# A GRU followed by a mixture of experts: shared experts for two blocks at a time, 32x32 turns on VectorE, logits by column groups, first loads in another order

## The chip, the cores and the metric

The kernel runs on one core of a Trainium2 chip. The metric is the device time of one execution in microseconds; smaller is better. The core has five engines that work side by side: TensorE (PE, with its weight loads PEld), VectorE (DVE), ScalarE (ACT), GpSimd (POOL) and SyncE (SP), which issues most DMAs. Each works through its own list of instructions in order, and semaphores make one wait for another.

## The reference, cut to what matters

```python
def cell(h, x):                      # 256 steps, 8 sequences, width 512
    gi = x @ W_ih + b_ih
    gh = h @ W_hh + b_hh
    r = sigmoid(i_r + h_r)
    z = sigmoid(i_z + h_z)
    n = tanh(i_n + r * h_n)
    return (1 - z) * n + z * h
...
x_ = hs.reshape(-1, 512)             # 2048 tokens
probs = softmax(x_ @ w_gate)         # 8 experts, the best 2, their weights made to sum to 1
gu = einsum('th,ehf->etf', x_, w_gate_up)
eo = einsum('eti,eih->eth', silu_and_mul(gu), w_down)
routed = einsum('te,eth->th', combine, eo)
shared = silu_and_mul(x_ @ w_sh_gate_up) @ w_sh_down
return x + (routed + shared)
```

Everything is float32. The GRU is a chain of 256 dependent steps; the experts need only the states.

## The kernel before, in words

Time is cut into 16 blocks of 16 steps (8 sequences x 16 steps = 128 tokens). In each block the 16 steps are issued one after the other, and between a step's last gate and the next step's first gate TensorE is given other work, "pieces" from a queue. A planner at the end of the file gives each piece a cost (`MM = 0.86` for four matmuls of 512 columns or their like) and hands out pieces so that the block's sum is even over its steps. The order on each engine is the order of the program.

A step (`step`, L379 to L418): three gates r, n, z of 16 matmuls each, with the turned state (8 columns) as weights and a 128-column slice of W_hh moving, into four groups of 32 columns of the array. Then VectorE turns each gate's result by 32x32 blocks (L390), ScalarE makes r, nn and z (L398, L406, L409), VectorE makes the new state hT (L402 to L415), GpSimd copies it into `hc` (L418). The input part of the gates ("seeds") is put into the gates' PSUM banks by ScalarE (`open_gate`, L366).

The other work:
- `project` (L283, tile gip): x @ W_ih of a later block, 12 pieces a block. The result gi gets its bias on VectorE (L321), goes to DRAM, and comes back in another layout, four steps at a time, as the seeds (`load_seeds` L350, `turn_seeds` L354).
- `transpose_x` (L270, tile xTp): x of a later block turned by four full 128x128 transposes on TensorE, copied by ScalarE (L272).
- `shared_unit` (L670, tile gu_s): the shared experts of the block before. Four units a block, each four "up" pieces (16 matmuls of 32 weight columns and 128 moving tokens), a gate on ScalarE and VectorE (L598 to L600), two "down" pieces (L283, tile po).
- routing of the block before: `choose` (L430, tile lgp: logits, 128 weight columns, 8 moving columns), `order_experts`, `weigh`, `give_places` (L483, L485), `enter` (indirect DMAs into lists), `send_rows` (L523, tile hrp: the states turned back on TensorE, copied by ScalarE, sent to DRAM).

After the last step the last block's shared experts run while the lists of tokens are finished (the shared tail), and then 39 tiles of 128 tokens go through the chosen experts (L606, L742), each gathered and added back by indirect DMAs.

At the start x of block 0 comes by ScalarE's queue, W_ih in three 1 MB DMAs and W_hh in four by SP's, and the two biases spread over 128 partitions by GpSimd's queue; then block 0 is projected, its seeds go to DRAM and back, and the first step starts.

Of the kernel before, what the change touches and what calls it, by code (L numbers as in the profile page):

```python
# [17 lines left out]
P = 128  # L18
TS = 16
SC = 4  # L20
NS = 2
# [4 lines left out]
def kernel(  # L26
# [45 lines left out]

    nc = tc.nc
# [21 lines left out]
    three = ctx.enter_context(tc.tile_pool(name="three", bufs=2))  # L95
# [3 lines left out]
    ps_t = ctx.enter_context(tc.tile_pool(name="ps_t", bufs=1, space=PSUM))  # L99
    ps_o = ctx.enter_context(tc.tile_pool(name="ps_o", bufs=1, space=PSUM))  # L100
# [3 lines left out]
    x_tiles = {}  # L104

    def load_x(k, queue=nc.sync):
        xt = xpool.tile([P, D], F32, tag="x", name=f"x_{k}")
        queue.dma_start(xt, x[:, k * TS : (k + 1) * TS, :])
        x_tiles[k] = xt

    load_x(0, nc.scalar)
# [4 lines left out]
    whh = we[:, E - 4 : E - 2].rearrange("p e w n -> p (e w n)").rearrange("p (q n) -> p q n", q=NQ)  # L116
    for g in range(3):
        nc.sync.dma_start(
            wih[:, :, g * D : (g + 1) * D],
            w_ih[:, g * D : (g + 1) * D].rearrange("(q p) n -> p q n", p=P),  # L120
        )
    bias = const.tile([P, G3], F32, name="bias")
    nc.gpsimd.dma_start(bias, b_ih.partition_broadcast(P))
    bias_h = we[:, 0, 0:2].rearrange("p w n -> p (w n)")
    nc.gpsimd.dma_start(bias_h, b_hh[0 : 2 * D].partition_broadcast(P))
    h = state.tile([P, NQ, 32], F32, name="h")
    nc.vector.memset(h, 0.0)
    h0v = h0.rearrange("b (q j i) -> b j q i", q=NQ, j=4)
    for j in range(4):
        nc.gpsimd.dma_start(h[32 * j : 32 * j + B], h0v[:, j])  # L130
    for q in range(NQ):
        nc.sync.dma_start(whh[:, q, :], w_hh[q * P : (q + 1) * P, :])
    load_x(1)
    wg = wts.tile([P, NQ, E], F32, name="wg")
# [7 lines left out]
    def load(tile_, src):  # L142
        loads.append(lambda: nc.gpsimd.dma_start(tile_, src))

    def load_shared():
        load(wg, w_gate.rearrange("(q p) e -> p q e", p=P))
        up = w_sh_gate_up.rearrange("(q p) (two c f) -> p q two c f", p=P, two=2, f=IM)
        down = w_sh_down.rearrange("(c f p) n -> c p f n", p=P, f=NF)
        for c in range(NSH):
            for two_i in range(2):  # L150
                for q in range(0, NQ, 2):
                    load(wsu[c][:, q : q + 2, two_i, :], up[:, q : q + 2, two_i, c, :])
            for f in range(NF):
                load(wsd[c][:, f, :], down[c][:, f, :])

    def load_expert(e):
        for q in range(NQ):
            load(we[:, e, q, :], w_gate_up[e, q * P : (q + 1) * P, :])
        for f in range(NF):
            load(we[:, e, NQ + f, :], w_down[e, f * P : (f + 1) * P, :])  # L160
# [26 lines left out]
    def counting(name, n, base, step, channel):  # L187
# [24 lines left out]


# [8 lines left out]
    nc.vector.tensor_tensor(  # L222
        bias[:, 0 : 2 * D], bias[:, 0 : 2 * D], bias_h, ALU.add
    )
    b_hn = b_hh[2 * D : G3].rearrange("(q j i) -> j q i", q=NQ, j=4)
    for j in range(4):
        nc.gpsimd.dma_start(
            seed_hn[32 * j : 32 * j + B].rearrange("p (q i) -> p q i", i=32),
            b_hn[j].partition_broadcast(B),
        )  # L230
# [9 lines left out]
    nc.gpsimd.dma_start(listed[0 : E * NM], vacant)  # L240
    nc.gpsimd.dma_start(listed[E * NM : E * NM + 1], vacant[0:1])
# [13 lines left out]
    by_groups = [True]  # L255
    spare = deque()

    def for_transposes(shape, name):

        if by_groups[0]:  # L260
            return ps_t.tile([P, *shape], F32, tag="tp", name=name)
# [5 lines left out]
    def transpose_x(k):  # L267
        ps = for_transposes([NQ, P], f"xTp_{k}")
        for q in range(NQ):
            nc.tensor.transpose(ps[:, q, :], x_tiles[k][:, q * P : (q + 1) * P], ident)  # L270
        xT = two.tile([P, NQ, P], F32, tag="xrT", name=f"xT_{k}")
        nc.scalar.copy(xT, ps)  # L272
        xT_of[k] = xT
        x_tiles.pop(k)
# [3 lines left out]
    def multiply(ps, lhs, rhs, start, stop):  # L278


        for c in range(4) if by_groups[0] else (slice(0, P),):
            rows_ = slice(32 * c, 32 * c + 32) if by_groups[0] else c
            nc.tensor.matmul(  # L283
                ps[rows_], lhs[:, rows_], rhs, start=start, stop=stop, skip_group_check=True
            )

# [18 lines left out]
    def project(k, g):  # L305
# [3 lines left out]
        def issue(q, cols):  # L309
            if q == 0 and cols.start == 0:  # L310
# [3 lines left out]
                xT_of[k][:, q, :],  # L314
# [5 lines left out]
        def end():  # L320
            nc.vector.tensor_tensor(  # L321
                gi[:, :, g, :].rearrange("p j (q i) -> p j q i", i=32),
                box["ps"].rearrange("p (q j i) -> p j q i", j=4, i=32),
                bias[:, g * D : (g + 1) * D].rearrange("p (q j i) -> p j q i", j=4, i=32),
                ALU.add,
            )
            if g > 0:
                to = gi_dram[k][g % 2].rearrange("j b t n -> (b t) j n")
                if g == 1:
                    nc.sync.dma_start(to.rearrange("p j (a n) -> p j a n", a=2), gi[:, :, 0:2, :])  # L330
                else:
                    nc.sync.dma_start(to, gi[:, :, 2, :])
                    projected.add(k)
# [9 lines left out]
    def load_seeds(c):  # L343

        k, o = divmod(c * SC, TS)
        assert k in projected
        steps = slice(o, o + SC)
        for tile_, src in zip((seeds_n, seeds[c % NS]), gi_dram[k]):
            for j in range(4):
                nc.sync.dma_start(tile_[32 * j : 32 * j + B], src[j, :, steps, :])  # L350
    def turn_seeds(c):
# [16 lines left out]
    whh_v = whh.rearrange("p q (a j i) -> p q a j i", j=4, i=32)  # L368
    hc_of = {}

# [566 lines left out]
```

## Time and profile before

| what | us |
|---|---|
| median of 3 runs (lowest, highest) | 1541.06 (1536.35, 1541.35) |
| profiled execution, its own time | 1539.5 |
| its span, from first to last instruction | 1537.7 |
| first step's first gate starts at | 35.46 |
| last step's first gate starts at | 1262.83 |
| first matmul for the last block's logits | 1267.21 |
| first transposition of a token tile | 1295.81 |

The span is what the trace covers; the profiled execution's time lies 1.8 us above it. A row of the stage view gives a stretch, its length, each engine's busy time with the count of instructions, the granted TensorE clock (1.00 is full), the share of DMA time and GB/s. A line of the timeline gives start, duration, engine, line, operation and tiles, shapes and count, and in brackets the idle time before and what ended it. A matmul's record is 0.27 us or longer, since matmuls overlap: what one costs is the distance between starts, not its duration. A float32 matmul appears as two instructions. In places the records are displaced by a few instructions, so that the last ones of one group bear the next group's name.

### The profile page before, as it was taken

To read this page: it belongs to the slowest core of one execution; us is meant where nothing else is said; L and a number is where in the kernel's file an instruction comes from. 1 tells how busy PE (TensorE), PEld (TensorE's weight loads), DVE (VectorE), ACT (ScalarE), POOL (GpSimd) and SP (SyncE) were. 2 spreads that over 40 slices of the span, in tenths; PEclk is the share of its full clock that TensorE was granted. 3 is DMA by queue.
4 is the path that set the end of the run, shared out by engine and by line. 5 is a ranking of instruction groups with operands and counts; after the bars stand their busy time and mean duration, and the time that the engine had idled before them with its cause. 6 is when DMAs were issued, how large, how long until landed. Compare 5 with 4: busy or idle time off the path is not lost.

```text
span 1537.7 us, 82219 instructions
## 1 busy us (share of the span) xinstructions
PE 1472.1 (96%) x36779; PEld 1156.5 (75%) x36779; DVE 732.9 (48%) x2747; ACT 435.5 (28%) x1799; POOL 253.7 (16%) x492
## 2 busy tenths in 40 slices
PE   4999799999999999999999999999999999999996
PEld 1777678887889897879897979797889886444442
DVE  2555354545455555555555555555455553222221
ACT  1332232333233323333323333333233331222221
POOL 2112111111110000000001010101010213444442
PEclk9999999999999999999999999999999999999998
DMA  7334122322221111111111110101010224455453
GB/s 255 91 104 105 29 55 50 81 49 82 48 61 29 45 32 45 32 39 31 40 37 30 40 41 22 48 21 48 21 48 22 70 64 142 85 94 90 89 96 48
DMA packets 52720, 94.51 MB, mean 61 GB/s; under 512 B 9152, under 2 KB 25616, under 8 KB 52368
## 3 DMA queue, kind: packets, MB, share of 16 engines
q0 software_dynamic: 16416, 41.00, 12.7%
q1 hardware_dynamic: 35816, 47.99, 11.2%
q8 instruction: 290, 4.75, 1.3%
q14 instruction: 62, 0.51, 0.1%
q10 hardware_dynamic: 136, 0.26, 0.1%
HBM read 57.85 MB, written 31.37 MB: 58 GB/s over the span
## 4 chain that ended last, share of the span: by engine, by line
PE 94%; issue 2%; DMA 1%; DVE 1%; ACT 0%; SPq 0%; POOLq 0%; POOL 0%; DVEq 0%; ACTq 0%
PE ps_r L379 15%; PE ps_n L379 15%; PE gu_s L670 15%; PE ps_z L379 15%; PE gip L283 11%; PE gu_t L606 9%; PE po L283 7%; PE yp L742 4%; PE lgp L430 1%; DMA x<-in_x_dram 1%; PE xTp L270 1%; PE hrp L523 1%; PE ps_r L723 0%; PE ps_z L723 0%; PE ps_n L723 0%
## 5 line engine op out<-in xcount | busy, mean ns | idle before, releaser
L379 PE MATMUL ps_r<-we,hT 128*8 128x128 f32 x8192 | 292.7, 274 | 15.4 <-ACT ps_r L366 9.1
L379 PE MATMUL ps_z<-we,hT 128*8 128x128 f32 x8192 | 295.0, 273 | 6.8 <-issue 6.2
L379 PE MATMUL ps_n<-we,hT 128*8 128x128 f32 x8192 | 295.8, 273 | 4.7 <-issue 4.2
L379 PEld LDWEIGHTS ps_r<-we,hT 128*8 128x8 f32 x8192 | 240.5, 90 | 73.9 <-issue 30.1
L670 PE MATMUL gu_s<-hc,wsu 128*32 128x128 f32 x8192 | 280.7, 275 | 10.3 <-issue 10.0
L670 PEld LDWEIGHTS gu_s<-hc,wsu 128*32 128x32 f32 x8192 | 252.5, 111 | 30.9 <-issue 22.1
L379 PEld LDWEIGHTS ps_z<-we,hT 128*8 128x8 f32 x8192 | 241.2, 90 | 11.8 <-issue 10.8
L379 PEld LDWEIGHTS ps_n<-we,hT 128*8 128x8 f32 x8192 | 240.7, 90 | 11.0 <-issue 9.3
L418 POOL COPY hc<-hT 128x32 f32<-128x32 f32 x256 | 62.2, 243 | 1076.1 <-DVE hT L415 1076.1
L398 ACT ACTIVATE r<-rT 128x32 f32<-128x32 f32 x256 | 58.6, 229 | 566.7 <-DVE rT L390 564.5
L390 DVE STREAM_TRANSPOSE rT<-ps_r 128x128 f32<-128x128 f32 x256 | 81.0, 316 | 264.5 <-PE ps_r L379 263.5
L283 PE MATMUL gip<-we,xT 128*32 128x512 f32 (+1 forms) x1904 | 190.6, 517 | 1.5 <-ACT xT L272 1.5
L390 DVE STREAM_TRANSPOSE nT<-ps_n 128x128 f32<-128x128 f32 x256 | 81.2, 317 | 144.3 <-PE ps_n L379 144.2
L606 PE MATMUL gu_t<-we,xrT 128*128 x312 | 146.7, 593 | 0.2 <-ACT xrT L725 0.2
L283 PE MATMUL po<-wsd,act_s 128*32 128x512 f32 (+2 forms) x1108 | 138.4, 539 | 1.7 <-DVE act_s L600 1.7
L283 PEld LDWEIGHTS gip<-we,xT 128*32 128x32 f32 x1904 | 58.9, 110 | 67.6 <-issue 56.5
L366 ACT COPY ps_n<-seed_hn 128x128 f32<-128x128 f32 x256 | 68.9, 269 | 104.5 <-DVE nT L390 103.4
L390 DVE STREAM_TRANSPOSE zT<-ps_z 128x128 f32<-128x128 f32 x256 | 81.1, 317 | 18.2 <-PE ps_z L379 10.4
L599 DVE TENSOR_TENSOR act_t<-gu_t,act_t 128x256 f32<-128x256 f32 x39 | 16.6, 425 | 146.3 <-ACT act_t L598 146.3
L606 PEld LDWEIGHTS gu_t<-we,xrT 128*128 128x128 f32 x312 | 53.3, 190 | 38.7 <-issue 38.0
L406 ACT ACTIVATE nn<-nt 128x32 f32<-128x32 f32 x256 | 58.8, 229 | 82.8 <-DVE nt L404 80.5
L748 POOL DMA_INDIRECT out_dram<-y,row x39 | 61.5, 1578 | 124.7 <-DVE y L745 111.1
(162 smaller groups left out, 1231.8 us busy)
## 6 DMA issues: line engine op xcount, KB each, us to landing
gid_rz<-gi SPq DMA_DIRECT2D x16, 512.0 KB
seeds<-gid_rz SPq DMA_DIRECT2D x256, 32.0 KB
we<-in_L_ffn_w_gate_up_dram POOLq DMA_DIRECT2D x32, 256.0 KB, 3.7
gid_n<-gi SPq DMA_DIRECT2D x16, 256.0 KB
seeds_n<-gid_n SPq DMA_DIRECT2D x256, 16.0 KB
wsu<-_L_ffn_w_sh_gate_up_dram POOLq DMA_DIRECT2D x16, 256.0 KB, 3.2
rows<-hr SPq DMA_DIRECT2D x16, 256.0 KB
again<-in_x_dram SPq DMA_DIRECT2D x16, 256.0 KB
```

The source lines that it names most:

```text
L283: nc.tensor.matmul(ps[rows_], lhs[:, rows_], rhs, start=start, stop=stop, skip_group_check=True)
L366: nc.scalar.copy(banks[g][:, 0:P], src[g])
L379: nc.tensor.matmul(bank[32 * j : 32 * j + B, 0:P].rearrange("p (a i) -> p a i", i=32), hT[:, q, 0:B], whh_v[:, q, lo : lo + NQ, j, :], sta ...
L390: nc.vector.transpose(gT.rearrange("p a b -> p (a b)"), banks[g][:, 0:P])
L398: nc.scalar.activation(r, gr, AF.Sigmoid)
L406: nc.scalar.activation(nn, nt, AF.Tanh)
L418: nc.gpsimd.tensor_copy(hc_of[k].rearrange("p q (b t) -> p q b t", t=TS)[:, :, :, t], new)
L599: nc.vector.tensor_tensor(act, ps[:, 0:IM], act, ALU.mult)
L606: nc.tensor.matmul(box["ps"], lhs(q), w_up(q), start=(q == 0), stop=(q == NQ - 1))
L670: nc.tensor.matmul(box["ps"][32 * g : 32 * g + 32, m, :], wsu[c][:, q, two_i, fs], hc_of[k][:, q, :], start=(m == 0 and q == 0), stop=(q = ...
L742: nc.tensor.matmul(box["y"], lhs, rhs, start=(f == 0), stop=(f == NF - 1))
L748: nc.gpsimd.indirect_dma_start(out=out.rearrange("b t d -> (b t) d"), out_offset=bass.IndirectOffsetOnAxis(ap=laid["row"][:, i : i + 1], a ...
```

## The change

- Shared experts run for a pair of blocks: `hc` holds two blocks, an up piece has 256 moving tokens, there are eight units a pair, each half of the former in weights, issued four in each of the two following blocks. The down pieces of a unit are issued after the up pieces of the second unit after it (`down_later`), with three buffers for act and two PSUM banks for po. The last pair runs after the last step.
- x and the states are turned by VectorE in 32x32 blocks. For that, the width is split as (j, q, i) instead of (q, j, i), by strided DMAs of x, W_ih, W_hh, w_gate, w_sh_gate_up and rows in parts of 16 or 32 partitions (`by_turns`, `by_state`), x and rows in runs of 512 bytes.
- The logits are made by four matmuls side by side, one for each q, each with 32 weight columns (w_gate, filled with zeros), and summed by a second, small matmul one step later (`sum_logits`). `give_places` goes by column groups too.
- The first loads: x first, in eight parts on two queues, W_ih by gates, x of block 1 before W_hh, W_hh by gates. The lists' first values are written from the queue of loads. Biases are loaded as one row and spread by a matmul with a row of ones. The first four projection pieces of block 1 go ahead of the first step.

```diff
-    load_x(0, nc.scalar)
+    load_x(0, (nc.sync, nc.scalar))
...
+    nc.scalar.dma_start(bias_row, b_ih.unsqueeze(0))
+    nc.scalar.dma_start(bias_h, b_hh[0 : 2 * D].unsqueeze(0))
     for g in range(3):
...
+        for ps, src in by_state(w_ih[:, cols]):
+            nc.sync.dma_start(wih[ps, :, cols], src)
...
+    def spread_bias(g):
+        ps = ps_mm.tile([P, D], F32, tag="mm", name=f"biasp_{g}")
+        cols = slice(g * D, (g + 1) * D)
+        nc.tensor.matmul(ps, one, bias_row[:, cols], start=True, stop=True)
+        nc.scalar.copy(bias[:, cols], ps)
...
     def transpose_x(k):
-        ps = for_transposes([NQ, P], f"xTp_{k}")
-        for q in range(NQ):
-            nc.tensor.transpose(ps[:, q, :], x_tiles[k][:, q * P : (q + 1) * P], ident)
-        xT = two.tile([P, NQ, P], F32, tag="xrT", name=f"xT_{k}")
-        nc.scalar.copy(xT, ps)
+        xT = two.tile([P, NG, NQ, 32], F32, tag="xrT", name=f"xT_{k}")
+        nc.vector.transpose(
+            xT.rearrange("p g q s -> p (g q s)"), x_tiles.pop(k).rearrange("p g m -> p (g m)")
+        )
...
         for q in range(NQ):
-            nc.tensor.matmul(ps, hc[:, q, :], wg[:, q, :], start=(q == 0), stop=(q == NQ - 1))
-        lg = two.tile([P, E], F32, tag="lg", name=f"lg_{k}")
-        nc.scalar.copy(lg, ps)
+            nc.tensor.matmul(
+                ps[32 * q : 32 * q + 32, 0:P], wg[:, q, :], hc[:, :, q, :], start=True, stop=True
+            )
+        parts = two.tile([P, P], F32, tag="parts", name=f"parts_{k}", bufs=1)
+        nc.scalar.copy(parts, ps[:, 0:P])
+        lg_of[k] = ps, parts
+
+    def sum_logits(k):
+        ps, parts = lg_of[k]
+        multiply(ps[:, P : P + E], columns(parts), sel, start=True, stop=True)
...
-        for q in range(NQ):
-            nc.tensor.transpose(ps[:, q * P : (q + 1) * P], hc[:, q, :], ident)
-        hr = two.tile([P, D], F32, tag="y", name=f"hr_{k}")
-        nc.scalar.copy(hr, ps)
-        nc.sync.dma_start(rows[:, k * TS : (k + 1) * TS, :], hr)
+        hr = two.tile([P, NG, P], F32, tag="y", name=f"hr_{k}")
+        nc.vector.transpose(
+            hr.rearrange("p g m -> p (g m)"), hc_of_block(k).rearrange("p g q s -> p (g q s)")
+        )
+        for ps, dst in by_turns(rows, k):
+            nc.sync.dma_start(dst, hr[ps])
...
-                        box["ps"][32 * g : 32 * g + 32, m, :],
+                        box["ps"][32 * g : 32 * g + 32, two_i, :],
                         wsu[c][:, q, two_i, fs],
-                        hc_of[k][:, q, :],
+                        hc_of[m][:, :, q, :],
...
-        quota = 2.8 * PROJECT if k == 0 else sum(p[0] for p in projections) / max(1, NB - 1 - k)
+        quota = 33 * MM if k < 2 else sum(p[0] for p in projections) / max(1, NB - 1 - k)
...
-        if k > 0:
-            for c in range(NSH):
-                feed_at_once(shared_unit(k - 1, c, NSH))
+        if k > 1:
+            half = NSH * NF // 2
+            for u in range(half):
+                feed_shared(k // 2 - 1, half * (k % 2) + u)
...
-    for c in range(NSH):
-        feed_at_once(shared_unit(k, c, NSH))
+    for u in range(NSH * NF):
+        feed_shared(k // 2, u)
+    while down_later:
+        queue.extend(down_later.popleft())
```

## The prediction

> **What bounds the kernel now.** I read the page first: TensorE is busy almost all of the span and the chain of waits is TensorE for 94%.
>
> ```profile
> span 1537.7 us, 82219 instructions
> ...
> PE 1472.1 (96%) x36779; PEld 1156.5 (75%) x36779; DVE 732.9 (48%) x2747; ACT 435.5 (28%) x1799; POOL 253.7 (16%) x492
> ...
> q8 instruction: 290, 4.75, 1.3%
> ...
> PE 94%; issue 2%; DMA 1%; DVE 1%; ACT 0%; SPq 0%; POOLq 0%; POOL 0%; DVEq 0%; ACTq 0%
> ```
>
> The reader is to see that fewer TensorE microseconds should be a shorter span, unless something else waits behind TensorE. To look for that I cut the span into stages: start-up to 35.46, sixteen blocks of 16 GRU steps to 1262.83 plus a last step, the shared tail to 1295.8, the expert tiles.
>
> ```profile
> 35.46:111.00 75.54, 74.74 (x1880) 54.37 (x1884) 37.71 (x139) 24.72 (x103) 14.27 (x32) 0.98 0.31 93
> 111.00:199.36 88.36, 77.17 (x2233) 65.02 (x2226) 40.69 (x163) 23.17 (x104) 18.19 (x34) 0.98 0.29 66
> 199.36:1195.80 996.44, 982.88 (x29167) 842.27 (x29167) 533.90 (x2101) 307.92 (x1363) 89.35 (x259) 1.00 0.17 42
> 1195.80:1262.80 67.00, 63.81 (x2042) 56.45 (x2035) 36.54 (x151) 21.93 (x98) 11.85 (x29) 1.00 0.29 76
> 1267.20:1295.80 28.60, 26.76 (x550) 19.27 (x551) 9.67 (x43) 2.59 (x8) 12.54 (x18) 1.00 0.57 164
> 1295.80:1537.70 241.90, 227.28 (x703) 110.77 (x701) 63.12 (x118) 52.28 (x117) 97.29 (x75) 0.98 0.47 83
> ```
>
> Columns: stretch and length, busy PE, PEld, DVE, ACT, POOL, then clock, DMA share, GB/s. The 996.44 row holds the 208 steps of blocks 2 to 14, 4.79 each; block 15 (67.00, fifteen steps) has less other work and takes 4.47 a step. Block 1 (88.36) has TensorE idle for 11.2 us. The timeline of one step in the middle gives the law:
>
> ```profile
> 900.43 1.06 PE L379 MATMUL ps_r<-we,hT 128*8 128x128 f32 x32
> 901.31 1.06 PE L379 MATMUL ps_n<-we,hT 128*8 128x128 f32 x32
> 902.18 1.06 PE L379 MATMUL ps_z<-we,hT 128*8 128x128 f32 x32
> 903.05 1.90 PE L283 MATMUL gip<-we,xT 128*32 128x512 f32 x16
> ...
> 904.27 0.19 DVE L415 TENSOR_TENSOR hT<-nn,hn 128x32 f32<-128x32 f32 x1
> ...
> 904.77 1.06 PE L379 MATMUL ps_r<-we,hT 128*8 128x128 f32 x32
> ```
>
> Three gates start 0.87 apart, 2.62 in all; two projection pieces fill 1.72 (0.86 each); the new state was there at 904.46, before the fill ended. A step is 2.62 + F, F being the fill. In block 15 F is only 1.3:
>
> ```profile
> 1243.41 1.06 PE L379 MATMUL ps_z<-we,hT 128*8 128x128 f32 x32
> ...
> 1244.28 1.50 PE L670 MATMUL gu_s<-hc,wsu 128*32 128x128 f32 x48
> 1244.53 0.32 DVE L390 STREAM_TRANSPOSE zT<-ps_z 128x128 f32<-128x128 f32 x1
> ...
> 1245.50 0.19 DVE L415 TENSOR_TENSOR hT<-nn,hn 128x32 f32<-128x32 f32 x1
> ...
> 1245.83 1.06 PE L379 MATMUL ps_r<-we,hT 128*8 128x128 f32 x32
> ```
>
> From 1241.66 to 1245.83 the step is 4.17: TensorE waits for hT. So a step is max(2.62 + F, 4.17), and fill below 1.55 buys nothing. This floor decides the case.
>
> [...] 0.873 / 8 = 109 ns per set of four column groups at N = 128, 0.86 / 2 = 430 at N = 512. [...] steps whose fill has a full-array piece (xTp, hrp) run 0.3 us over the law. [...] TensorE stops for 2 to 4 us inside a run with no wait shown ("issue"). [...] here 0.711 for 128x512 (seeds_n row).
>
> **The change, part by part.** I count against the profiled execution (span 1537.7, time 1539.5, so 1.8 around it; 1.6 under the median 1541.06).
>
> *Shared experts, two blocks at once.* 16 matmuls of 256 columns take the place of two sets of 128. [...] the trace, 109 at 128 and 430 at 512, gives 215 to 218. That is 2% of 8192 x 27.3 ns = 224 us, below 5 us; I take 0 and keep -5. An up piece now lasts 1.72 and is still booked at 0.86, so fill gets uneven.
>
> *Full-array work leaves TensorE.* Per block: xTp 4 x 0.107 + 0.3 = 0.73, gone; hrp 0.73, gone; lgp 1.25 [...] becomes four 128-column matmuls side by side, 0.22, and eight of 8 columns, 0.2 at most; posp 0.28 becomes 0.2. Fifteen times (0.73 + 0.73 + 0.83 + 0.08) = 35.5 us of fill less. In their place VectorE gets two 0.711 turns a block, and ACT two 0.58 copies fewer. The turns stand behind hT on VectorE; what is queued behind them is rT of the next step, due 1.06 after its r gate starts, with 0.56 to spare before nt. One turn fits in that; with gi (0.69) or gated work (0.84) ahead, or the seeds' turn beside weigh (0.91), it can pass it. Bounds: 0 to 1 us a block; I take 0.35, 5 us in all.
>
> *Moved work.* Block k's shared experts wait for the pair: one block (24 x 0.86 = 20.6) and 3.0 of late down pieces go from under the GRU into the tail. Four projection pieces (3.4) go ahead of the first step. Fill falls by 35.5 + 20.6 + 3.0 + 3.4 = 62.5, from 514 to 452.
>
> *What the floor gives back.* The changed kernel's instruction order on TensorE, built, gives the fill after each step. In blocks 6 to 14 it is 1.53, 1.07, 1.31, 1.31, 1.51, 1.75, 2.62, 1.31, 2.19, 2.19, 2.19, 2.62, 1.31, 2.19, 2.19, 1.31: eight of sixteen under 1.55. Filling them up to the floor costs 1.9 a block, 3.5 in block 2, 4 in block 15: 31 us over the kernel, against 3 before (block 15 alone). So the GRU gains 62.5 - 28 = 34.5.
>
> *Stalls.* The law gives 1178 for the 1227.4 from first to last step start; 49 are stalls, 15 of them in block 1, where wsu's loads meet the eight list entries. The loads stay; block 1 now has only 512-column pieces, 16 matmul instructions in 1.72 instead of 64, so fewer to fetch, and x and rows go in 512-byte pieces, eight DMAs instead of one. With VectorE's 5 I take 42, range 27 to 60.
>
> *SP's queue.* Per block 32 seed loads of 0.33 stay, x and rows grow from 2 issues to 16: 5 us more in a 72 us block. Seeds are fetched a chunk of four steps (17 us) ahead; hidden.
>
> *Start-up.* Now x lands at 11.84 behind 3 MB of W_ih and 1.3 MB of spread biases, the projection runs 13.7 to 26.4, and the round trip of the seeds lasts to 35.46:
>
> ```profile
> 11.98 1.08 PE L270 MATMUL xTp<-ident,x 128*128 128x128 f32 x4 [8.20 <-DMA x<-in_x_dram]
> ...
> 27.19 0.37 SPq L332 DMA_DIRECT2D gid_n<-gi  x1
> ```
>
> Changed: x first, biases as two rows, W_ih by gates. 1.3 MB less and one gate (1 MB) instead of three before the first matmul: I put the start at 7 to 8. Twelve pieces 10.3, three bias matmuls 2.6[...]: end about 22.5; the four moved pieces to 26. The seeds of r and z: gi at 19, then 0.4 + 2.96 + 1.3 + 2.2 as today: 26. First step 26.5, 9 earlier (bounds 23 and 31). n's seeds come about 2 late for step 0, as the first step's 2.7 stall now.
>
> *Tail.* Pieces before the first tile: 16 up of 1.72 and 20 down of 0.86 = 44.7, choose, places, lists 2.1; waits 2 (3.3 now; the longer cover should hide some): 48.8 against 28.6, +20.2. Tiles unchanged, 241.9.
>
> Sum: -34.5 - 7 (stalls) - 9 + 20.2 = -30; span 1507, time **1508**.
>
> **Rivals.** *More gain:* the stalls fall to 27, start 3 us earlier, the 5 us of the longer matmuls come: 1485. For it: instruction fetch has less to do, and no mode switch is left. Against: half the steps stand on the floor and would keep what is gained under them. *Slower, by one mechanism:* VectorE's queue between hT and the next rT lengthens the chain, so that the floor is 4.5 instead of 4.17. The same sum with 4.5 gives 44 us more, 1552; it decides from 4.43 on (33 us more). For it: the added turns, and eight steps a block with no slack. Against: order_experts and weigh (1 us of VectorE) already stand there and cost nothing in filled steps; block 15 lost only 0.3 in such steps. *No change:* floor near 4.4, 1537, because what leaves TensorE was cover. *The change doesn't do what it says:* the longer moving operand alone brings next to nothing, as above; my forecast already says that the gain is from the removed full-array work and the start.
>
> **How the numbers follow.** Forecast 1508 (1493 to 1523): 0.62. More gain: 0.22. Floor near 4.4: 0.06. Floor 4.5 and over: 0.10. The range 1484 to 1536 holds the first two and the better part of the third. A measurement can't tell less than 0.3% (4.6 us) from none: faster 0.86, same 0.04, slower 0.10.
>
> **What would show it.** Right: first r gate near 26; no xTp and hrp; unfilled steps of 4.2 and filled ones at the law; blocks of 72 to 75; gu_s near 218 ns per set of 256 columns; tail near 49. Wrong: unfilled steps at 4.4 or more with rT late, blocks 0 and 1 above 85, or a first step after 31.

## The result, and the profile after

The changed kernel took 1515.51 us in the median of 4 runs (1514.79 to 1517.33), the kernel before 1539.19 (4 runs, three of them those of the table above, 1536.35 to 1541.35): a ratio of 0.985, 95% interval 0.983 to 0.987. It is about 24 us faster, where the forecast had 33 under the earlier median, 31.5 under the profiled execution. The kernel before is less steady from one measurement to another than within one: beside the experiments its median was 1521 to 1535. The profiled execution took 1514.91, its span is 1513.1.

These lines of the page after answer to those shown of before: span, engines, instruction fetch (packets, MB, share), the chain by engine.

```profile
span 1513.1 us, 75290 instructions
...
PE 1443.1 (95%) x33154; PEld 1058.3 (70%) x33154; DVE 751.6 (50%) x2782; ACT 423.4 (28%) x1786; POOL 258.6 (17%) x505
...
q8 instruction: 261, 4.28, 1.2%
...
PE 90%; DMA 3%; DVE 3%; issue 2%; ACT 1%; SPq 0%; ACTq 0%; POOLq 0%; DVEq 0%; POOL 0%
```

TensorE has 3625 instructions and 29 us less. Its share of the chain fell from 94% to 90%, and DMA and VectorE have 3% each instead of 1%: something ahead of TensorE has become longer. The stage view says where (stretch and length; busy PE, PEld, DVE, ACT, POOL; clock, DMA share, GB/s). The stretches are block 0, block 1, blocks 2 to 14, block 15 up to its last step, the tail from the last block's logits on, and the tiles:

```profile
55.06:126.31 71.25, 71.25 (x1895) 57.19 (x1891) 40.37 (x144) 20.82 (x96) 19.15 (x45) 1.00 0.39 107
126.31:204.06 77.75, 74.66 (x1883) 58.44 (x1878) 42.88 (x163) 21.40 (x100) 21.89 (x42) 1.00 0.42 89
204.06:1154.76 950.70, 932.69 (x25941) 747.26 (x25938) 541.20 (x2116) 297.82 (x1352) 89.76 (x259) 1.00 0.15 41
1154.76:1219.99 65.23, 62.39 (x1808) 51.08 (x1809) 37.40 (x151) 21.52 (x98) 12.19 (x30) 1.00 0.28 73
1224.38:1271.60 47.22, 47.13 (x701) 23.56 (x701) 14.69 (x54) 3.80 (x12) 12.61 (x18) 1.00 0.41 116
1271.60:1513.10 241.50, 227.33 (x703) 110.92 (x702) 63.11 (x118) 52.33 (x117) 97.35 (x75) 0.98 0.48 84
```

The first number matters most: the first gate starts at 55.06, where it was 35.46 before and 26.5 in the forecast. Everything behind it went as forecast or better:

| stretch (us) | before | forecast | after | after less forecast |
|---|---|---|---|---|
| start to first r gate | 35.46 | 26.5 | 55.06 | +28.6 |
| first to last step's start | 1227.4 | 1185.9 | 1164.9 | -21.0 |
| last step's start to last logits | 4.4 | 4.4 | 4.4 | 0 |
| logits to first tile | 28.6 | 48.8 | 47.2 | -1.6 |
| tiles | 241.9 | 241.9 | 241.5 | -0.4 |
| span | 1537.7 | 1507.5 | 1513.1 | +5.6 |

So a time 7.5 us from the forecast hides two errors of 20 to 30 us with opposite signs. (The forecast's own parts add up to a span of 1507.5, a time of 1509.3 with the 1.8 around it; the 1508 written there is 1.3 short of its sum.) The start is read from the timeline of the changed kernel (start, duration, engine, line, operation, tiles, in brackets the idle time before and its releaser):

```profile
10.74 5.35 PE L310 MATMUL gip<-we,xT 128*32 128x512 f32 x24 [6.82 <-DMA we<-in_L_cond_W_ih_dram]
...
20.11 8.94 SPq L152 DMA_DIRECT2D we<-in_L_cond_W_hh_dram  x12
...
23.00 0.69 DVE L356 TENSOR_TENSOR gi<-gip,bias 128x512 f32<-128x512 f32 x1 [3.93 <-PE gip L310]
...
29.93 8.69 SPq L119 DMA_DIRECT2D x<-in_x_dram  x8
38.73 0.40 SPq L366 DMA_DIRECT2D gid_rz<-gi  x1
...
48.03 0.71 DVE L391 STREAM_TRANSPOSE nT<-seeds_n 128x512 f32<-128x512 f32 x1 [19.72 <-DMA seeds_n<-gid_n]
48.67 0.67 DVE L299 STREAM_TRANSPOSE xT<-x 128x512 f32<-128x512 f32 x1
...
49.48 5.76 PE L310 MATMUL gip<-we,xT 128*32 128x512 f32 x32 [22.00 <-DVE xT L299]
...
55.06 1.06 PE L419 MATMUL ps_r<-we,hT 128*8 128x128 f32 x32
```

gi of r and z is complete at 23.7, but its DMA to DRAM is issued only at 38.73: on SP's queue the twelve parts of W_hh (20.11 to 29.05) and the eight parts of x of block 2 (29.93 to 38.62) stand ahead of it. Of the 8.69 us of x 6.9 are waiting for an earlier DMA to land, as the waits of SP's queue show (us in total, times, longest); of the 8.94 of W_hh it is 3.2:

```profile
SPq L119 <- DMA we<-in_L_cond_W_hh_dram: 6.9, 8, 1.0
```

Then comes the round trip; and VectorE turns n's seeds before x of block 1, so that the four moved projection pieces run alone, from 49.48 on, and the first gate waits for them. They take 5.76 us. TensorE stood still for 22.00 before them, and its granted clock, 1.00 in each us up to 29, is 0.50 from 30 to 53 and 1.00 again from 54 on; the pieces' weight loads start 0.86 apart up to 53.73 and 0.43 apart at their end.

The weights themselves came late too. The same stage view for 10 to 20 us, of before:

```profile
10.00:20.00 10.00, 7.35 (x44) 2.37 (x48) 1.85 (x4) 0.59 (x1) 2.51 (x5) 1.00 1.04 390
```

and after:

```profile
10.00:20.00 10.00, 9.26 (x54) 2.46 (x58) 0.82 (x2) 0.59 (x1) 0.00 (x0) 1.00 1.03 206
```

The DMA engines are as busy (1.04 and 1.03), but move 206 GB/s instead of 390. Packets of 2048 bytes took 84 ns in the median of this stretch before and 165 ns after. The changed kernel loads the two matrices in parts of 32 partitions, the kernel before over all 128, a difference that the prediction did not price. Whether it is the cause had to be tried.

In the steps the floor stayed where it was. A step of block 8 after, with 1.3 us of fill, in the timeline:

```profile
649.29 1.06 PE L419 MATMUL ps_r<-we,hT 128*8 128x128 f32 x32
650.16 1.06 PE L419 MATMUL ps_n<-we,hT 128*8 128x128 f32 x32
651.03 1.06 PE L419 MATMUL ps_z<-we,hT 128*8 128x128 f32 x32
651.90 0.23 PE L310 MATMUL lgp<-sel,parts 128*32 128x8 f32 x8
651.97 1.06 PE L310 MATMUL gip<-we,xT 128*32 128x256 f32 x16
653.46 1.06 PE L419 MATMUL ps_r<-we,hT 128*8 128x128 f32 x32 [0.44 <-DVE hT L455]
```

From 649.29 to 653.46 it is 4.17, the floor of before, and TensorE's last wait is for hT: VectorE's added turns did not lengthen the chain. By the law of the prediction, max(2.62 + F, 4.17), the steps after add up to 1144.2; they took 1164.9, so that the stalls are 20.7, where they were 49 and 42 had been forecast.

### The profile page after: what moved, and what is told of

Same layout as the page of the kernel before. It is cut to its first block, busy times and chain, and to the rows that moved or that the text cites. A ratio compares the mean times of both kernels' runs of the same rounds, so it can differ in the third digit from the quotient of the medians.

```text
span 1513.1 us, 75290 instructions
## 1 busy us (share of the span) xinstructions
PE 1443.1 (95%) x33154; PEld 1058.3 (70%) x33154; DVE 751.6 (50%) x2782; ACT 423.4 (28%) x1786; POOL 258.6 (17%) x505
## 4 chain that ended last, share of the span: by engine, by line
PE 90%; DMA 3%; DVE 3%; issue 2%; ACT 1%; SPq 0%; ACTq 0%; POOLq 0%; DVEq 0%; POOL 0%
PE ps_r L419 16%; PE ps_n L419 15%; PE gu_s L705 15%; PE ps_z L419 14%; PE gu_t L659 9%; PE gip L310 9%; PE po L310 7%; PE yp L785 4%; DMA we<-in_L_cond_W_hh_dram 1%; DVE zT L430 1%; DMA we<-in_L_cond_W_ih_dram 1%; DVE hn L454 0%; ACT z L449 0%; DVE hT L455 0%; PE ps_z L766 0%
## 5 line engine op out<-in xcount | busy, mean ns | idle before, releaser
L419 PEld LDWEIGHTS ps_r<-we,hT 128*8 128x8 f32 x8192 | 226.1, 89 | 119.3 <-ACT ps_z L403 72.7
L419 PE MATMUL ps_r<-we,hT 128*8 128x128 f32 x8192 | 280.8, 273 | 18.4 <-DVE hT L455 11.3
L419 PE MATMUL ps_n<-we,hT 128*8 128x128 f32 x8192 | 288.6, 273 | 1.0 <-issue 0.4
L419 PE MATMUL ps_z<-we,hT 128*8 128x128 f32 x8192 | 283.7, 273 | 2.4 <-issue 2.4
L705 PE MATMUL gu_s<-hc,wsu 128*32 128x256 f32 x4096 | 250.6, 379 | 1.2 <-issue 1.1
L419 PEld LDWEIGHTS ps_n<-we,hT 128*8 128x8 f32 x8192 | 233.6, 90 | 8.3 <-issue 7.5
L310 PE MATMUL gip<-we,xT 128*32 128x512 f32 (+1 forms) x1976 | 197.2, 508 | 29.5 <-DVE xT L299 22.0
L705 PEld LDWEIGHTS gu_s<-hc,wsu 128*32 128x32 f32 x4096 | 150.9, 110 | 76.0 <-issue 14.6
L310 PE MATMUL po<-wsd,act_s 128*32 128x256 f32 (+1 forms) x1408 | 137.9, 476 | 0.0
L310 PEld LDWEIGHTS gip<-we,xT 128*32 128x32 f32 x1976 | 73.7, 111 | 82.0 <-issue 63.9
```

What stands on the lines that cost most here:

```text
L310: nc.tensor.matmul(ps[32 * c : 32 * c + 32], lhs(c), rhs, start=start, stop=stop, skip_group_check=True,)
L419: nc.tensor.matmul(bank[32 * j : 32 * j + B, 0:P], hT[:, q, 0:B], whh_v[:, q, a, j, :], start=False, stop=(q == NQ - 1), skip_group_check= ...
L705: nc.tensor.matmul(box["ps"][32 * g : 32 * g + 32, two_i, :], wsu[c][:, q, two_i, fs], hc_of[m][:, :, q, :], start=(two_i == 0 and q == 0) ...
```

## The experiments

Three questions: what makes the first gate late, why the steps lost more stalls than forecast, and whether the floor is what it seemed. "First gate" is the start of the first r gate. Single executions are read by their stages; times measured apart are compared by their ratio to the kernel before, which ran beside each. The first two experiments, the up pieces of 128 tokens and the dummy work were measured beside one another (before 1533.36), so were the two queues, the later turn, the full booking and the two together (before 1521.39), and so were the run over all partitions and the last one (before 1535.46).

### Start: block 0's gi and seeds on GpSimd's queue

```diff
-                    nc.sync.dma_start(to.rearrange(...), gi[:, :, 0:2, :])
+                    (nc.gpsimd if k == 0 else nc.sync).dma_start(to.rearrange(...), gi[:, :, 0:2, :])
...
-                nc.sync.dma_start(tile_[32 * j : 32 * j + B], src[j, :, steps, :])
+                (nc.gpsimd if c < NS else nc.sync).dma_start(tile_[32 * j : 32 * j + B], src[j, :, steps, :])
```

> The changed kernel, but block 0's gi and its first two chunks of seeds go by GpSimd's queue instead of SP's. Theory A (place in SP's queue: gi of z was ready at 23.7 us and its DMA was issued at 38.7, behind the issues of W_hh and of two x blocks): the seeds of r and z are there near 31, the first r gate starts near 31 to 36 instead of 55. Theory B (the loads themselves are slow: 32 partitions at a time, 160 to 206 GB/s in the start-up windows against 290 to 390 before): W_hh still lands near 38, so the gates of the first step are held apart by W_hh, n and z not before 33 and 38; the first step ends near 40. If A alone holds, the second step starts by 37; if B holds too, near 41. Either way 14 to 20 us less in all, about 1496 to 1501.

Measured: 1505.75 (before 1533.36), first gate 52.76. gi now leaves SP's queue out, as the timeline shows:

```profile
24.46 0.83 POOL L366 DMA_DIRECT2D gid_rz<-gi  x1 [17.56 <-DVE gi L356]
...
35.02 2.05 POOL L386 DMA_DIRECT2D seeds<-gid_rz  x4 [9.73 <-DMA gid_rz<-gi]
...
42.31 0.27 ACT L403 COPY ps_r<-seeds 128x128 f32<-128x128 f32 x1 [14.72 <-DMA seeds<-gid_rz]
```

It is issued 14.3 us earlier, but lands only at 35, after 10.5 us, while the DMA engines are full with W_hh and x (share 1.07 from 30 to 40 us); in the changed kernel it lands by 41.6, 3 us after its issue. The seeds of r and z then take 7.3 us by this queue until ScalarE copies them (42.31), against 3.6 by SP's (41.64 to 45.21). The first gate gains 2.3 us, not 19 or more: a miss. Getting out of SP's queue does not by itself free the step. How much the place in the queue costs with an equally fast queue this run doesn't tell.

### Start: W_ih and W_hh over 128 partitions in one DMA each

```diff
-        for ps, src in by_state(w_ih[:, cols]):
-            nc.sync.dma_start(wih[ps, :, cols], src)
+        src = w_ih[:, cols].rearrange("(j q i) n -> q j i n", j=4, i=32)
+        for q in range(NQ):
+            nc.sync.dma_start(wih[:, q, cols], src[q])
```

and the same for W_hh.

> The changed kernel, but W_ih and W_hh are loaded by 128 partitions at a time (one DMA for each gate and q, same bytes, same number of DMAs, same 2 KB runs), nothing else moved. Theory B [...]: 10 to 30 us shows 350 GB/s and more instead of 200, W_hh is there by about 24 instead of 38, SP's issues are held up less, and the first step starts near 38 to 42 instead of 55. Theory A alone (only the order of issues on SP matters, the number of issues is the same): GB/s as before and first step within 3 us of 55.

Measured: 1550.13, first gate 92.87. A miss, and not a test of what was meant. The stage view for 10 to 20 us:

```profile
10.00:20.00 10.00, 7.52 (x34) 1.51 (x34) 1.99 (x7) 1.87 (x2) 0.00 (x0) 1.00 0.26 98
```

A DMA share of 0.26 is the time of 0.26 x 16 = 4.2 engines, and j, the first dimension of each source here, has 4 values. The run of the next section has as many DMAs, as large and over as many partitions, with 128 successive rows as the source, and a share of 0.70 and 225 GB/s in the same stretch. So the rate goes with the form of the source; what in it does so was not shown, that it is j is an estimate from the 4.2. A packet of 2048 bytes took 87 ns, first evidence for the partitions, though with a quarter of the engines' time in use.

### Start: as many DMAs of the same size, over all partitions

```diff
-        for ps, src in by_state(w_ih[:, cols]):
-            nc.sync.dma_start(wih[ps, :, cols], src)
+        for q in range(NQ):
+            nc.sync.dma_start(wih[:, q, cols], w_ih[q * P : (q + 1) * P, cols])
```

and the same for W_hh.

> The changed kernel with W_ih and W_hh loaded by 128 contiguous rows at a time (one DMA for each gate and group of 128 rows: twelve DMAs of 256 KB for each matrix, as many and as large as in the changed kernel, with the same 2 KB runs, each DMA over all 128 partitions instead of 32). Rows of the two matrices stand in another order than the states expect, so the recurrence computes with permuted weights; sizes, counts and order of all work are unchanged. Theory A (a DMA into 32 partitions moves at half the rate): 2 KB packets take about 86 ns instead of 164, 350 to 400 GB/s in 10 to 20 us, gi of the r gate on its way by 30, first r gate at 38 to 46 instead of 55, whole time 1499 to 1508. Rival B (the number of DMAs and SP's waits for the DMA eight earlier set the pace, whatever their partitions): about 200 GB/s in 10 to 20 us, first r gate at 53 or later, time 1514 to 1517.

Measured: first gate 46.27, 8.8 us earlier; time 1509.27 (before 1535.46). 2 KB packets took 84 ns, and 337 GB/s were moved from 18 to 24 us (212 from 21 to 30 after); from 20 to 30 it is 270 at a DMA share of 0.79, where the changed kernel has 193 at 0.92. The timeline of this run:

```profile
8.84 5.35 PE L310 MATMUL gip<-we,xT 128*32 128x512 f32 x24 [4.91 <-DVE xT L299]
...
23.31 6.46 SPq L119 DMA_DIRECT2D x<-in_x_dram  x8
...
29.89 0.40 SPq L366 DMA_DIRECT2D gid_rz<-gi  x1
...
39.39 0.71 DVE L391 STREAM_TRANSPOSE nT<-seeds_n 128x512 f32<-128x512 f32 x1 [13.08 <-DMA seeds_n<-gid_n]
40.02 0.67 DVE L299 STREAM_TRANSPOSE xT<-x 128x512 f32<-128x512 f32 x1
...
40.84 5.62 PE L310 MATMUL gip<-we,xT 128*32 128x512 f32 x32 [15.37 <-DVE xT L299]
...
46.27 1.06 PE L419 MATMUL ps_r<-we,hT 128*8 128x128 f32 x32
```

gi's DMA is issued 8.84 earlier, and all behind it moves along: 2.0 of this is gi itself (z added by 21.7 instead of 23.7), 6.8 the shorter wait on SP's queue. With number, size, queue and order of the DMAs the same, and 2 KB packets in both, the partitions of each differ, and with them the rows that it reads: the half rate is shown, and costs 8.8 us at the start. Theory A held, the sizes were a little too hopeful (46.27 against at most 46; the time is 1.3 over its range, and block 1 took 81.5 in this execution instead of 77.8). The expected 350 to 400 GB/s in 10 to 20 us did not come (225): W_ih had landed by 15.5, and W_hh was issued only from 16.54 on.

### Start: the two halves of the partitions on two queues

```diff
-        for ps, src in by_state(w_ih[:, cols]):
-            nc.sync.dma_start(wih[ps, :, cols], src)
+        for j, (ps, src) in enumerate(by_state(w_ih[:, cols])):
+            (nc.sync if j < 2 else nc.scalar).dma_start(wih[ps, :, cols], src)
```

and the same for W_hh.

> The changed kernel, but of W_ih's and W_hh's parts the upper two groups of 32 partitions (64 to 127) go by ScalarE's queue and the lower two by SP's, side by side; the parts themselves are unchanged. Theory B [...]: the window 10 to 20 us shows 330 GB/s and more instead of 206, W_hh is there by about 24 instead of 38, gi's DMA for r and z is issued near 26 instead of 38.7, first r gate 36 to 42 instead of 55, in all 13 to 18 us less (near 1500). Rival (runs of 2 KB in parts of 256 KB are slow by their size, whatever partitions): GB/s within 20% of 206, first gate within 4 us of 55.

Measured: 1500.68 (before 1521.39), first gate 50.78 instead of 36 to 42. The rate hardly rose. The stage view of the changed kernel for 20 to 30 us:

```profile
20.00:30.00 10.00, 7.48 (x52) 1.68 (x44) 1.38 (x2) 1.17 (x2) 0.00 (x0) 1.00 0.92 193
```

and of this run for 10 to 20 and 20 to 30:

```profile
10.00:20.00 10.00, 7.73 (x50) 2.14 (x54) 0.33 (x1) 0.00 (x0) 0.00 (x0) 1.00 0.86 184
20.00:30.00 10.00, 3.50 (x18) 0.83 (x14) 1.00 (x2) 2.07 (x3) 0.00 (x0) 0.78 0.98 244
```

In the stretch that the forecast named, 10 to 20, it is 184 instead of the expected 330 (206 in the changed kernel). From 22 to 28, where W_hh lands and the engines are full in both, it is 244 against 222 (323 in the run over all partitions). So two DMAs of 32 partitions side by side, one in each half, did not do here what one over all 128 does. And ScalarE's copies of the bias now stand behind its issues of W_hh:

```profile
25.76 1.28 ACT L260 ACT_TABLE_LOAD   x1 [25.76 <-DMA we<-in_L_cond_W_hh_dram]
27.05 0.59 ACT L260 COPY bias<-biasp 128x512 f32<-128x512 f32 x1
```

and gi of z, which needs the bias, is added at 32.5 instead of 23.7; its DMA leaves at 34.34. A miss in rate and first gate; the time fell near its forecast, but the kernel before was shorter here as well, and the ratio of this one execution, 0.986, shows no gain over 0.985. The issues were put ahead of work on ScalarE that I had not counted.

### Start: in addition, n's seeds turned behind x and the four pieces

```diff
-    turn_seeds(0)
-    load_seeds(1)
     load_shared()
...
     for g in banks:
         open_gate(0, g)
+    turn_seeds(0)
+    load_seeds(1)
```

> e5_two_queues, and VectorE's turn of n's first seeds goes behind the turn of x of block 1 and the four moved projection pieces, which it stood ahead of. Theory C (in the changed kernel the four pieces waited for that turn, 49.5 to 55, so that they were on the way to the first step instead of beside it): the pieces run right behind block 0's projection, first r gate near 29 to 33, the second step's r gate near 34 to 37, 4 to 6 us less than e5_two_queues. Rival (x of block 1 comes late anyway): within 2 us of e5_two_queues.

Measured: 1494.52, first gate 42.09, 8.7 earlier than with the two queues alone. The timeline:

```profile
37.81 0.70 DVE L299 STREAM_TRANSPOSE xT<-x 128x512 f32<-128x512 f32 x1
...
38.66 3.64 PE L310 MATMUL gip<-we,xT 128*32 128x512 f32 x32 [1.59 <-DVE xT L299]
...
42.09 1.08 PE L419 MATMUL ps_r<-we,hT 128*8 128x128 f32 x32
```

The pieces start while the seeds of n are still on their way, and take 3.64 instead of 5.76; their weight loads start 0.43 apart, and the granted clock is 1.00 from 40 to 50 us, where it was 0.50 in the changed kernel. The order on VectorE (with the next seeds' loads, which move along with the turn) is worth 8.7 us of the first gate here, and 6.2 us of the time. The gate came 9 us later than forecast (29 to 33), since gi of z and n came late with the bias, as with the two queues alone, and on VectorE the turn of x stands behind them (37.81).

### Steps: the up pieces as two matmuls of 128 tokens again

```diff
-                    nc.tensor.matmul(
-                        box["ps"][32 * g : 32 * g + 32, two_i, :],
-                        wsu[c][:, q, two_i, fs], hc_of[m][:, :, q, :], ...)
+                    for b in range(2):
+                        nc.tensor.matmul(
+                            box["ps"][32 * g : 32 * g + 32, two_i, b * P : (b + 1) * P],
+                            wsu[c][:, q, two_i, fs], hc_of[m][:, NG * b : NG * b + NG, q, :], ...)
```

> The changed kernel, but each up piece's matmul of 256 tokens is two of 128 (4096 more matmul instructions and weight loads; all else as in the changed kernel). The law of steps asks 2 to 3% of 224 us, 4 to 6 us less what stands under the floor. Theory I (the stalls without a named wait, 49 us before and 21 in the changed kernel, come from the number of TensorE instructions to fetch): 15 to 28 us slower than the changed kernel, 1530 to 1543, the excess over the law near 40. Theory II (they fell because the loads now meet other work in block 1 and because nothing full-array is left): 3 to 6 us slower, 1518 to 1522.

Measured: 1543.28 in the median of 5 runs (1530.54 to 1551.34), ratio to before 1.008 (1.005 to 1.011), against 0.985 of the changed kernel: 2.3% for an edit that leaves work and order alone. From the page of this run:

```profile
PE 1450.9 (95%) x37250; PEld 1143.1 (75%) x37250; DVE 750.5 (49%) x2782; ACT 423.4 (28%) x1786; POOL 257.8 (17%) x505
...
q8 instruction: 293, 4.80, 1.4%
```

The 4096 instructions are back, and with them the fetched blocks: 293 (before 290, after 261). The profiled execution is the fastest of the five; its steps took 1180.2, and 1161.3 and 1163.0 in the first two experiments, which were measured beside it and have the steps of the changed kernel. Of these 17 to 19 us no more than 5 are the shorter matmuls themselves: a set of four column groups with 256 tokens takes 216 ns after, two with 128 tokens 2 x 109 before, 1% more, which is some 2 us of 224. The other 12 to 14 are stalls that no wait names. They are uneven, as a longer piece would not be: block 15 took 68.6 instead of 65.6 and 64.1, blocks 2 and 3 together 151.1 instead of 146.3 and 145.8. So the stalls go with the number of TensorE instructions (each of these matmuls brings a weight load, and the two aren't told apart); that the fetch of instructions is what stalls them fits the counts, and was not tried by itself. It is also only about half of the 28 us by which the stalls fell from before to after. Another part lies in block 1, where TensorE's idle time fell from 11.2 to 3.1 us by the stage views (88.36 - 77.17, 77.75 - 74.66); which part of the change did that was not tried.

### Steps: 0.43 us of dummy work in known steps

```diff
+        def more_full(k=k):
+            ps = ps_mm.tile([P, NQ, P], F32, tag="mm", name=f"more_{k}")
+            for q in range(NQ):
+                nc.tensor.transpose(ps[:, q, :], ident, ident)
+
+        def more_groups(k=k):
+            ps = ps_mm.tile([P, 2 * P], F32, tag="mm", name=f"more_{k}")
+            multiply(ps, columns(ident), wsd[0][:, 0, 0 : 2 * P], start=True, stop=True)
+
+        if k > 5:
+            when((2, 9, 9)[k % 3], 0, (more_full, more_full, more_groups)[k % 3])
```

> The changed kernel with 0.43 us of unused TensorE work added to one step of each block from block 6 on: in blocks 6, 9, 12, 15 four full-array transposes after step 2 (fill 1.31, unfilled), in 7, 10, 13 the same after step 9 (fill 2.19), in 8, 11, 14 four grouped matmuls of 256 columns after step 9. By the law alone: step 2 rises from 4.17 by 0.16, step 9 by 0.43 in both forms. If a full-array piece drains TensorE on the way in and out: step 2 by 0.46, step 9 by 0.73 in blocks 7, 10, 13 and by 0.43 in 8, 11, 14. If the floor were not a floor of the chain: step 2 by 0.43 or 0.73 as well. In all 4 to 7 us.

Measured: 1515.52. An unfilled step (step 2) with full-array work went from 4.17 to 4.64; a filled one (step 9) from 4.78 to 5.51 with full-array work, and to 5.21 with the same time in column groups, alike in each of the blocks. In the timeline of a filled one:

```profile
612.10 1.06 PE L419 MATMUL ps_r<-we,hT 128*8 128x128 f32 x32
...
614.84 0.66 PE L888 MATMUL more<-ident 128*128 128x128 f32 x4
...
617.61 1.06 PE L419 MATMUL ps_r<-we,hT 128*8 128x128 f32 x32
```

5.51 = 4.78 + 0.43 + 0.30: the change to full-array work and back costs 0.30, as the prediction took it from before: the first of these matmuls starts 0.13 after the end of ps_z's 0.87, and what follows starts (615.42) 0.15 after their 0.43. Column groups are free of it (5.21 = 4.78 + 0.43). In the unfilled step, 1.31 + 0.73 = 2.04 of fill gives 2.62 + 2.04 = 4.66: law and floor hold together.

### Steps: an up piece booked at what it lasts

```diff
             return (
-                MM,
+                2 * MM,
                 lambda: up(two_i, range(NQ)),
-                [(MM / 2, lambda qs=qs: up(two_i, qs)) for qs in parts],
+                [(MM / 2, lambda q=q: up(two_i, [q])) for q in range(NQ)],
             )
...
-                if len(queue[0]) > 2 and room < 0.75 * MM:
+                if len(queue[0]) > 2 and room < queue[0][0] - 0.25 * MM:
...
-            spent += piece[0]
+            spent += min(piece[0], MM)
```

> The changed kernel with an up piece booked at what it takes (2 x 0.86, four parts of 0.43), so that the fill is even over a block's steps; the same work, no other change. By the law of steps with the floor of 4.17 the sum over the 255 steps falls from 1144 to 1118: 24 to 27 us faster than the changed kernel, 1488 to 1492; blocks 6 to 14 take 70.1 to 71 instead of 72.3. Rival (VectorE's and ScalarE's work after the up pieces lengthens the chain when no step has slack): blocks stay at 72, less than 8 us.

Measured: 1481.98 in the median of 4 runs (1478.61 to 1484.15), ratio 0.973 (0.971 to 0.975). Block 8 in the stage view:

```profile
610.00:680.00 70.00, 69.99 (x1995) 56.67 (x1987) 42.27 (x164) 22.81 (x104) 5.86 (x18) 1.00 0.15 39
```

TensorE is busy throughout. Blocks 8 to 10 take 70.0 each (after: 73.8, 72.3, 72.8); the first step starts at 54.98, as after, and the last 1130.7 later. How many stalls there are differs between runs measured apart, so I compare with the two-queue runs above, which were measured beside this one and whose steps are those of the changed kernel: 1155.7 and 1158.0. The gain is 25 to 27 us; the law gives 1118.4 instead of 1144.2, which is 26. By the ratios to the kernel before, 0.973 against 0.985, it would be 18 us, but these come from two measurements apart. So the forecast's 28 us given back to the floor were real in the main, and could be had again.

### Both, and a last step at the start

The two queues, the seeds turned later and the up pieces booked in full, together:

> e6_queues_turn and e7_even together. If start and floor are separate causes the two gains add: 1515 - 23 (start) - 26 (even fill) = 1466, within 5 us. If the start's gain is only moved into the first steps' waits for seeds: 1478 or more.

Measured: 1469.18 in the median of 4 runs (1466.41 to 1469.99), ratio 0.965 (0.963 to 0.967), first gate 42.75, steps 1131.7. The two gains add up; it is faster than both kernels. On top of it:

```diff
-    load_x(1)
     for g in (0, 2, 1):
...
+    load_x(1, (nc.sync, nc.scalar))
     wg = wts.tile([P, NQ, 32], F32, name="wg")
...
-        if k + 2 < NB:
+        if 0 < k < NB - 2:
             load_x(k + 2)
...
+    load_x(2)
     load_shared()
...
-        nc.scalar.copy(bias[:, cols], ps)
+        nc.vector.tensor_copy(bias[:, cols], ps)
```

> The run with both mends (W halves on two queues, seeds turned behind the first pieces, up pieces booked at twice the cost) and in addition the loads of x of blocks 1 and 2 behind W_hh and behind block 0's gi, and the bias row spread by VectorE instead of ScalarE, whose copies stood behind W_hh's issues. If the x loads and ScalarE's place hold the first step at 42.8, as I think: first r gate at 34 to 39, 4 to 8 us off 1469, so 1461 to 1466, ratio to the kernel before about 0.961. Rival (the DMA engines' bytes ahead of gi are the bound, W_hh must land first whatever the queues do): first r gate within 2 us of 42.8 and 1467 to 1471.

Measured: 1475.18 in the median of 4 runs, before 1535.46 beside it; ratio 0.961 (0.959 to 0.964), first gate 41.53. The theory fell: with these loads and ScalarE's copies out of the way the gate came within 2 us of 42.75, as the rival had it. The timeline shows what holds the step now:

```profile
28.18 0.40 SPq L366 DMA_DIRECT2D gid_rz<-gi  x1
...
34.34 0.71 DVE L299 STREAM_TRANSPOSE xT<-x 128x512 f32<-128x512 f32 x1 [4.82 <-DMA x<-in_x_dram]
...
35.20 6.52 PE L310 MATMUL gip<-we,xT 128*32 128x512 f32 x32 [6.44 <-DVE xT L299]
...
41.53 1.06 PE L419 MATMUL ps_r<-we,hT 128*8 128x128 f32 x32
```

gi goes out 6 us earlier than in the run before it, but the pieces now wait for x of block 1 and run with weight loads 0.85 apart, 6.5 us (granted clock 0.54 in 30 to 40 us, after 6.44 without a matmul). What one mend frees, the pieces take. The steps were 6.0 us longer than in the run before it; but they were measured apart: beside this run the kernel before was 14 us longer too (1535.46 against 1521.39) and the steps of the changed kernel took 1167.7 (the run over all partitions) against 1155.7 and 1158.0. As the intervals touch, whether this version is better than the last stays open; so does a start without the pieces ahead, which was not tried.

## Why the prediction was right, and where its steps were off

- **The step that failed: "First step 26.5, 9 earlier (bounds 23 and 31)."** It was 55.06, beyond both bounds and beyond the prediction's own sign of being wrong, "a first step after 31". Four terms of it fell, and their errors add up to the 28.6. (1) "gi at 19": the bias was added by 23.7, +4.7. W_ih let the first matmul start at 10.74 where "7 to 8" was put; I took today's rate, but the parts of 32 partitions come at half of it (206 GB/s, 390 before). Of the 4.7, 2.0 go with the rate (z added by 21.7 in the run over all partitions); 1.3 are that even there the first matmul waited for the turn of x until 8.84, and 1.4 that the pieces and bias matmuls of r and z then took longer than put. (The forecast's end at 22.5 has 2.2 in it for a stretch of 4.4 at half the pace, as before, where the pieces' weight loads start 0.86 apart up to 18.01 and 0.43 apart from 18.49 on; after, they start 0.85 apart up to 14.13 and 0.43 from 17.63 on. The granted clock reads 1.00 in both stretches.) (2) gi's DMA was put right behind gi; it left at 38.73, +15.0, behind W_hh and x of block 2 on SP's queue (8.2 in the run over all partitions). The prediction counted the issues of x for the steps, but not at the start, where each waits for an earlier DMA to land. (3) The round trip, 7 by the forecast for r and z, ran 9.3 to the turn of n's seeds, +2.3. (4) The four pieces were put beside it ("to 26"); with x's turn behind the seeds' turn on VectorE they came after it, +7.0 from 48.03 to 55.06; the half us that the forecast had left between seeds and step goes off. Of all this 8.8 us are shown to be the half rate (all partitions, DMAs as many and as large), 8.7 the order on VectorE in the version with two queues; they overlap with the queue's part. What of the rest an experiment could remove stays open: the earliest first gate of all runs is 41.53, 15 later than forecast.
- **The floor is 4.17 and stays.** Right: unfilled steps take 4.17 to 4.18, filled ones the law, in the changed kernel and with dummy work. VectorE's turns, put at 5 us, cost nothing that shows. (By the prediction's own list of fills, bringing eight steps up to the floor costs 1.74 a block, not 1.9; this changes its sum by about 2 us.)
- **"What the floor gives back."** Right in mechanism, and near in size: evening out the fill brought 26 us by the law, against 28 forecast.
- **"Full-array work leaves TensorE", with 0.3 for each change of mode.** Right: 0.30 measured with the dummy work (5.51 against 5.21).
- **"I take 42, range 27 to 60" for the stalls.** The term of the sum that was mis-sized: 20.7, below the range (and 12 to 24 in other runs with the same steps). With it goes "I take 0" for the shared experts' wide matmuls. As busy time they bring next to nothing, 216 ns a set instead of 2 x 109, which is 1% and not the 2% worked out; but with 4096 instructions fewer there are 12 to 14 us fewer stalls in executions measured beside one another; the rest of the miss stays open. The prediction named that in one block and did not carry it to all.
- **Tail and tiles.** Right: 47.2 against 48.8, 241.5 against 241.9.
- **Rivals.** A longer floor did not come. *More gain* came nearest with the stalls (27), and was furthest off with the start.

That the time fell near the forecast is luck: the stalls and the start missed in opposite directions, by 21 and 29 us. Only the middle of the sum, the law of the steps with its floor, was understood.

## What to carry to other kernels

When a load is cut into parts for a new layout, price it anew: ask how many partitions each part reaches (8.8 us here), how many issues stand on the queue, and what is behind them, above all in the start, where nothing covers it. When a law with a floor tells which steps are too short, lay the work evenly: here the planner's wrong cost for one kind of piece was worth some 25 us, as much as the whole change brought. And count matmul instructions, not only their busy time: 12% more of them made the kernel 2.3% longer here.

## What was not expected of the hardware

- DMAs into 32 partitions moved at half the rate with the engines just as busy: 206 GB/s at a share of 1.03 against 390 at 1.04 over 128, and 165 ns for a packet of 2048 bytes against 84 (10 to 20 us, after and before; 84 also in the run over all partitions). Two such DMAs at once, one in each half of the partitions, brought 244 GB/s instead of 222, against 323 over all 128 (22 to 28 us).
- DMAs whose source had 4 as its first dimension used 0.26 of the engines' time and moved 98 GB/s; as many of the same size from 128 successive rows used 0.70 and moved 225 (10 to 20 us).
- The same order of work with 12% more TensorE instructions (37250, after 33154) ran 2.3% longer by the ratios to the kernel before, without a wait to show for it, and spreads wider (1530.5 to 1551.3).
